# Re-pricing the planner of a four-layer graph kernel: copy times, transfer rate, a larger hold around LSTM steps, the last three batches closer together

## The chip, the cores and the metric

The kernel runs on one core of one Trainium2 chip. The metric is device time in microseconds from the first to the last instruction of one execution, as the median of repeated runs. A core has a tensor engine (PE; its weight loads are PEld in the profile), a vector engine (DVE), a scalar engine (ACT), a GpSimd engine (POOL) and a sync engine (SP), which here only issues transfers. Each engine works through its own list of instructions in order; semaphores order the engines among each other.

## The reference

There are 32 graphs (batches) of 512 nodes with 128 features each, and a symmetric 0/1 adjacency matrix per graph. Four layers follow each other, each reading `h = max(layernorm(x), 0)` and adding its result to `x`:

```
q, k, v = relu(h Wq + bq), relu(h Wk + bk), relu(h Wv + bv)
x = x + softmax_over_neighbours(q k^T) v                      # layer 0
dyn = conv1d(h[:, -128:]) + conv_b
A_norm = D^-1/2 (A + I) D^-1/2
x = x + sigmoid((A_norm h) lstm(dyn))                         # layer 1
for i in 0..3:                                                # layer 2
    src, dst = nodes ws + bs, nodes wd + bd
    nodes' = tanh([l2norm(A) src, nodes wn + bn, l2norm(A)^T dst] wu + bu)
    (layers 2 and 3 also read the earlier nodes)
x = x + nodes                                                 # end of layer 2
x = x + prelu(A (h W^T) + bias)                               # layer 3
```

The LSTM has 128 steps, each of which needs the state of the step before for all 32 graphs. It runs over the 128 features of the last 128 nodes, with 32 graphs side by side.

## The kernel before

`symmetric` does the work in three stages, each once per batch. `pass_1(b)` loads `x[b]` and the last 128 columns of the adjacency matrix, normalizes, transposes on PE (`ln_t`, L823), projects to k, q and v (L1098, L1114), writes k and h (`f_dkq`) and v (`f_dv`) to DRAM, computes attention for the last 128 nodes and the convolution that feeds the LSTM (L1166), whose result goes to `seq`. `lstm()` follows all 32 convolutions: per step three gates on PE (L1194, `f_z`), tanh on ACT (L1209), the cell update on DVE (L1216 to L1218), the fourth gate (`f_zo`), two more tanh on ACT and the new state on DVE (L1230), which the next step's gates read. `pass_2(b)` loads what pass 1 wrote and the other 384 columns, and computes attention for the other 384 nodes (L1248, L1257, L1266); it fills PE beside the LSTM. `rest(b)` does the remaining layers: it loads the whole adjacency matrix (`f_a`, 1 MB, two buffers), squares it to f32r with the degrees (L1318), aggregates (L1302), uses the LSTM's output (L1354, L1361), and then runs layer 2: four times a product (L1408, `f_py`), a split into two parts on ACT and DVE (L1284, L1285), an aggregation (L1302, `f_pa`), a multiply on DVE (L1415), a product (L1419) and tanh on ACT (L1423). Layer 3 is normalization, aggregation (`f_pg3` in the program), eviction (`f_gT`), a product (L1455), three elementwise instructions (L1458, L1459, L1461) and the store of `out` (L1463).

Layer 2 needs two transposes per batch: of its input (`f_xn_c` to `f_hT_c` or `f_T_c`) and of its output (`f_n4`). Batches in `MOVED` do them by transfer (`by_transfer`): a copy that takes each f32 apart into 16-bit halves (`f_hl`), a transposing transfer (L1059) and a copy that puts them together (`f_T`). The copies may run on ACT (L1053) or DVE (L1054). The other batches transpose on PE (L823) and evict.

The order of all this isn't written out. Each instruction, or short group of them, is given to `Plan` as an operation: the engines that it may run on with a price in microseconds each, a rank, what it reads and writes. `Plan.run` then lays the operations out one by one: on each engine it takes the operation that can start first, by rank among those that can start now; on operations with two engines it takes the one on which they end first. The prices thus set the order of every engine's list, and the choice between ACT and DVE. The times in the plan are used nowhere else: on the chip, each engine follows the list and waits for semaphores.

Three rules matter here:

- Ranks under 1000 are the LSTM's. When one is awaited on an engine (`expected`, `held`), a ready operation of another rank is passed over if it would end more than 0.1 us after the LSTM's operation could start.
- Operations of rank 30,000 and above (`rest`) get a due time: 12 per batch, minus what still lies behind the operation. The lower value goes first.
- A transfer occupies SP in the plan for `t_dma`, 0.1 us + its KB over a rate.

PSUM has 8 banks. A bank that takes a bias by a copy (`fill`) may need a marking matmul first (L910), depending on what the bank held. Sixteen warm-up matmuls of no use to the result (L898) stand at the start, and sixteen more after the last batch's transposes.

Of the kernel before, what the change touches and what calls it, by code (L numbers as in the profile page):

```python
# [520 lines left out]
class Plan:  # L521
# [67 lines left out]
    def run(self, tc, queues):  # L589
# [14 lines left out]
        for o in ops:  # L604
            if o.rank >= self.last:
                k, sub = divmod(o.rank - self.last, 10)
                o.rank = self.last + 12 * k + 200.0 - (min(behind[o], 60) if sub == 5 else behind[o] + (70 if sub == 2 else 0.0))
        free = {}
# [62 lines left out]
        while done < len(ops):  # L671
            best = None
            for e, cands in pools.items():
                first = None
                held = expected.get(e)
                for rank, no, o in cands:
                    r = room(o)
                    if r is None:
                        continue
                    if r:  # L680
                        r += self.HOP
                    s = max(free[e], o.ready[e], r)
                    if len(o.engines) > 1:
                        mine = s + o.engines[e][0]
                        if any(max(free[x], o.ready[x], r) + o.engines[x][0] < mine - 1e-9 for x in o.engines if x != e):
                            continue
                    if rank < self.URGENT:
                        held = s
                    elif held is not None and s < held < s + o.engines[e][0] - 0.1:
                        continue  # L690
                    if first is None or s < first[0] - 1e-9:
                        first = (s, o)
                        if s <= free[e] + 1e-9:
                            break
# [35 lines left out]
def symmetric(ctx, tc, x, adj, weights, cols, rows, lstm_b, prelu_a, out, fail):  # L730
# [20 lines left out]
    FOLDS = (4, 7, 10, 13)  # L751
    MOVED = range(3, B - 2)
    T_HALVES = 0.8
    TURN = 32
# [33 lines left out]
    def t_mm(n):  # L788
        return max(0.222, n * 0.001676)
# [12 lines left out]
    def t_dma(kb):  # L802
        return 0.1 + kb / 280.0

# [240 lines left out]
    def by_transfer(rank, src, c, tag, name):  # L1045
# [5 lines left out]

        def move(dst, src, r, w):
            return plan.op({"ACT": (T_HALVES, lambda: nc.scalar.copy(dst(), src())),  # L1053
                            "DVE": (1.05, lambda: nc.vector.tensor_copy(dst(), src()))}, rank, [r], [w])  # L1054

        apart = new("xn", (P, NT, 2, P), f"f_hl_{name}", U16)
        move(lambda: apart.t, lambda: halves(src()), c, apart)
        turned = new("gs", (P, 2 * NT, P), f"f_hT_{name}", U16)
        sent = plan.op({"SP": (1.3, lambda: nc.sync.dma_start_transpose(out=turned.t, in_=apart.t.rearrange("p t h n -> p (t h n)")))}, rank,  # L1059
                [apart], [turned], gap=3.0)  # L1060
        whole = new(tag, (P, N), f"f_T_{name}")
        move(lambda: halves(whole.t), lambda: turned.t.rearrange("p (t h) n -> p t h n", h=2), turned, whole)
        return whole, sent
# [110 lines left out]
    def lstm():  # L1174
# [23 lines left out]
        for t in range(T):  # L1198
# [7 lines left out]
            if t:  # L1206
                PE(R, 0.68, lambda z=z, k=k, t=t: states(z, k, (0, 1, 2), t), [], [z], after=last)
            th = new("th", (P, 4, B), f"f_th_{t}")
# [15 lines left out]
            if t:  # L1224
                PE(R, 0.23, lambda zo=zo, ko=ko, t=t: states(zo, ko, (3,), t), [], [zo], after=last)
            ACT(R, 0.13, lambda th=th, zo=zo, ko=ko: nc.scalar.activation(th.t[:, 3, :], zo.t[:, ko, 0, :], AF.Tanh), [zo],
# [80 lines left out]
    def rest(b, lw_after):  # L1307
# [79 lines left out]
        turned_d = new("dt", (P, TURN), f"f_dT_{b}")  # L1387
        DVE(R + 1, 0.18, lambda: nc.vector.transpose(turned_d.t, flat(dinv.t)), [dinv], [turned_d])
        ddi = plan.fixed(dram.tile([NT, P], FP, tag=f"i{b}", name=f"f_ddi_{b}"))
# [11 lines left out]
        for i, nch in enumerate(L2_CHUNKS):  # L1401
# [3 lines left out]
            def sent(py=py, i=i, nch=nch):  # L1405
                for j in range(NT):
                    for c, n in enumerate(CHUNKS[i]):
                        nc.tensor.matmul(py.t[:, j, :], nodes[n].t[:, bass.ts(j, P)], wf[:, W_F[i] + c, 0, :], start=False,  # L1408
                                         stop=(c == nch - 1), skip_group_check=True)
            PE(R, 4 * nch * t_mm(P), sent, [nodes[n] for n in CHUNKS[i]], [py])  # L1410
            parts = split(R, py, f"{b}_{i}")
# [182 lines left out]
```

## Time and profile before

| | |
|---|---|
| timed runs, median of 3 | 1375.77 us (1375.0 to 1376.33) |
| the profiled run | 1372.96 us, span of the profile 1371.2 us |
| TensorE clock granted, mean | 0.997 |
| PE in pass 1, first warm-up to the start of the last convolution's last matmul | 4.9 to 185.2 us |
| LSTM, first gates' tanh to last state | 187.8 to 497.0 us |
| last product of pass 2 on PE | 587.4 us |
| last matmul | 1361.3 us |
| end of the last vector instruction | 1363.7 us |

The page's first part gives each engine's busy time, its share of the span and its instructions. The windows view gives the same by stretches of time: start and end, length, busy time of PE, PEld, DVE, ACT and POOL with instructions, the granted clock, the DMA engines' share and GB/s. The ends of matmuls are modelled, so in some places the starts of neighbouring records tell more than durations. The waits view names who waited, on whose account, for how long in total, how often and for how long at most.

```
PE   8999999999999999999999999999999999999995
DVE  7888866666666678777777777677677677675753
ACT  5565644455444465666776777677677677675541
GB/s 246 244 262 245 261 266 262 262 163 183 164 147 153 166 156 165 157 155 106 144 132 131 142 128 131 154 123 127 150 139 120 148 133 130 147 131 78 66 35 27
```

These are rows of the page's second part: the span in 40 slices of 34 us, each digit the busy share in tenths.

### The profile page before, as it was taken

To read this page: it belongs to the slowest core of one execution; us is meant where nothing else is said; L and a number is where in the kernel's file an instruction comes from. 1 tells how busy PE (TensorE), PEld (TensorE's weight loads), DVE (VectorE), ACT (ScalarE), POOL (GpSimd) and SP (SyncE) were. 2 spreads that over 40 slices of the span, in tenths; PEclk is the share of its full clock that TensorE was granted. 3 is DMA by queue.
4 is the path that set the end of the run, shared out by engine and by line. 5 is a ranking of instruction groups with operands and counts; after the bars stand their busy time and mean duration, and the time that the engine had idled before them with its cause. 6 is when DMAs were issued, how large, how long until landed. Compare 5 with 4: busy or idle time off the path is not lost. (4 is left out here: it accounts for less than half of the span.)

```text
span 1371.2 us, 24258 instructions
## 1 busy us (share of the span) xinstructions
PE 1339.3 (98%) x8022; PEld 1079.1 (79%) x8024; DVE 976.3 (71%) x3259; ACT 824.8 (60%) x1958; POOL 370.5 (27%) x689
## 2 busy tenths in 40 slices
PE   8999999999999999999999999999999999999995
PEld 6888888888888877888778787787787787886873
DVE  7888866666666678777777777677677677675753
ACT  5565644455444465666776777677677677675541
POOL 4555411111010133333223233232232232231200
PEclk9999999999999999999999999999999999999998
DMA  7777888855545556764565565755765665753310
GB/s 246 244 262 245 261 266 262 262 163 183 164 147 153 166 156 165 157 155 106 144 132 131 142 128 131 154 123 127 150 139 120 148 133 130 147 131 78 66 35 27
DMA packets 284008, 215.22 MB, mean 157 GB/s; under 512 B 133464, under 2 KB 246368, under 8 KB 283872
## 3 DMA queue, kind: packets, MB, share of 16 engines
q1 hardware_dynamic: 266976, 196.79, 52.3%
q0 software_dynamic: 16896, 16.78, 7.8%
q8 instruction: 65, 1.06, 0.3%
q14 instruction: 71, 0.58, 0.1%
HBM read 125.84 MB, written 56.75 MB: 133 GB/s over the span
## 5 line engine op out<-in xcount | busy, mean ns | idle before, releaser
L1302 PE MATMUL f_pa<-f_ar,f_y 128*128 128x512 f32 x1024 | 284.3, 416 | 0.7 <-ACT f_y L1284 0.7
L1302 PEld LDWEIGHTS f_pa<-f_ar,f_y 128*128 128x128 f32 x1024 | 189.3, 189 | 60.5 <-issue 21.7
L1408 PE MATMUL f_py<-f_wf,f_n 128*128 128x128 f32 x1280 | 174.2, 276 | 0.8 <-ACT f_n L1423 0.8
L1408 PEld LDWEIGHTS f_py<-f_wf,f_n 128*128 128x128 f32 x1280 | 162.9, 192 | 13.9 <-issue 6.2
L1419 PE MATMUL f_pa<-f_n,f_wf 128*128 128x512 f32 x320 | 154.6, 598 | 2.1 <-DVE f_pa L1415 1.5
L1423 ACT ACTIVATE f_n<-f_pa,f_bcol 128x512 f32<-128x512 f32 x128 | 87.8, 686 | 81.5 <-PE f_pa L1419 81.3
L1376 POOL DMA_DIRECT2D f_das<-f_ar x32 | 30.8, 962 | 358.9 <-DVE f_ar L1345 358.1
L1285 DVE TENSOR_TENSOR f_y<-f_py,f_y 128x512 fp32r<-128x512 f32 x128 | 87.3, 683 | 36.5 <-ACT f_y L1284 36.0
L1194 PEld LDWEIGHTS f_z<-f_seq,f_w 128*128 128x128 f32 x762 | 95.7, 192 | 22.0 <-DVE f_seq L1230 20.7
L1415 DVE TENSOR_TENSOR f_pa<-f_pa,f_inv 128x512 f32<-128x512 f32 x128 | 87.5, 693 | 34.3 <-PE f_pa L1302 34.3
L1266 PEld LDWEIGHTS f_po<-f_v,f_e 128*128 128x128 f32 x768 | 99.7, 192 | 14.8 <-issue 0.5
L1266 PE MATMUL f_po<-f_v,f_e 128*128 128x129 f32 x768 | 107.9, 279 | 0.0
L1345 DVE TENSOR_TENSOR f_ar<-f_ar,f_ident 128x512 fp32r<-128x512 f32 x64 | 43.7, 683 | 88.5 <-PE f_pg L1302 78.8
L1194 PE MATMUL f_z<-f_seq,f_w 128*128 128x32 f32 x762 | 101.0, 270 | 2.2 <-DVE f_seq L1230 1.1
L1026 ACT ACTIVATE f_xn_c<-f_x,f_sh_c,f_rs_c 128x128 f32<-128x128 f32 x167 | 71.2, 486 | 50.0 <-DVE f_sh_c L1034 50.0
L1257 PE MATMUL f_s<-f_q,f_kq 128*128 128x384 f32 x256 | 99.7, 501 | 0.0
L1419 PEld LDWEIGHTS f_pa<-f_n,f_wf 128*128 128x128 f32 x320 | 55.8, 190 | 50.5 <-issue 37.0
L1284 ACT CAST f_y<-f_py 128x512 fp32r<-128x512 f32 x128 | 74.1, 579 | 29.7 <-PE f_py L1408 25.5
L1277 POOL COPY f_ln<-f_mv_r 128x3 f32<-128x3 f32 x32 | 10.5, 330 | 287.1 <-DVE f_mv_r L1008 287.1
L828 ACT ACTIVATE f_gT<-f_pg 128x512 f32<-128x512 f32 x60 | 36.0, 600 | 80.4 <-PE f_pg L1302 80.4
L1209 ACT ACTIVATE f_th<-f_z 128x96 f32<-128x96 f32 x128 | 32.0, 250 | 83.0 <-PE f_z L1194 80.8
L1318 ACT ACTIVATE f_ar<-f_a 128x512 fp32r<-128x512 f32 x128 | 79.5, 624 | 2.7 <-DMA f_a<-in_adj_dram 2.7
(205 smaller groups left out, 3024.7 us busy)
## 6 DMA issues: line engine op xcount, KB each, us to landing
f_a<-in_adj_dram SPq DMA_DIRECT2D x32, 1024.0 KB
f_a<-in_adj_dram SPq DMA_DIRECT2D x32, 768.0 KB
f_das<-f_ar POOLq DMA_DIRECT2D x32, 512.0 KB, 5.1
f_dkq<-f_kh SPq DMA_DIRECT2D x32, 448.0 KB
f_kq<-f_dkq SPq DMA_DIRECT2D x32, 448.0 KB
f_dv<-f_v SPq DMA_DIRECT2D x32, 258.0 KB
f_v<-f_dv SPq DMA_DIRECT2D x32, 258.0 KB
f_x<-in_x_dram SPq DMA_DIRECT2D x32, 256.0 KB
```

Of the source, the lines that this page charges most:

```text
L1026: nc.scalar.activation(xn.t[:, t, :], xc.t[:, t, :], AF.Relu, bias=shift(t), scale=rstd(t))
L1194: nc.tensor.matmul(z.t[:, k, i, :], w[:, W_HH + q, :], seq[:, t - 1, :], start=False, stop=True, skip_group_check=True)
L1257: PE(R, t_mm(NR), lambda s=s, j=j: nc.tensor.matmul(s.t, kq.t[:, bass.ts(j, P)], q.t, start=True, stop=True), [kq, q], [s])
L1266: PE(R, t_mm(P), lambda t=t, j=j: nc.tensor.matmul(po.t[:, t, :], es[j].t[:, bass.ts(t, P)], v.t[:, j, :], start=(j == 0), stop=(j == NT - ...
L1284: ACT(rank, t_act(N), lambda: nc.scalar.copy(parts.t[:, :, 0, :], src.t), [src], [(parts, 0)])
L1285: DVE(rank, t_dve(N), lambda: nc.vector.tensor_sub(parts.t[:, :, 1, :], src.t, f32(parts.t[:, :, 0, :])), [src, (parts, 0)], [(parts, 1)])
L1302: nc.tensor.matmul(pg.t, parts.t[:, j, k, :], ar.t[:, j, :], start=(k == 0 and j == 0), stop=(k == 1 and j == NT - 1))
L1318: ACT(R, 0.62, lambda t=t: nc.scalar.activation(ar.t[:, t, :], a.t[:, t, :], AF.Square, accum_out=deg.t[:, t : t + 1]), [a], [(ar, t), (de ...
L1408: nc.tensor.matmul(py.t[:, j, :], nodes[n].t[:, bass.ts(j, P)], wf[:, W_F[i] + c, 0, :], start=False, stop=(c == nch - 1), skip_group_chec ...
L1415: before = DVE(R, t_dve(N), lambda pa=pa: nc.vector.tensor_mul(pa.t, pa.t, inv_row.t), [inv_row], [pa])
L1419: nc.tensor.matmul(pa.t, wf[:, W_F[i] + c, 1, :], nodes[n].t, start=False, stop=(c == nch - 1), skip_group_check=True)
L1423: ACT(R, 0.57, lambda pa=pa, n=n, i=i: nc.scalar.activation(n.t, pa.t, AF.Tanh, bias=bcol[:, i : i + 1]), [pa], [n])
```

## The change

The computation stays as it is, but for one batch more that transposes by transfer. What changes is the planner's input and two of its rules:

- in `Plan.run`, the due times of the last three batches are drawn together: 3 apart instead of 12;
- a ready operation may end up to 0.2 us, instead of 0.1, after an LSTM operation could start;
- `MOVED` takes in batch 2;
- the transfer rate is 315 KB per us instead of 280;
- the copies of `by_transfer` have prices of their own: 0.94 (ACT) and 0.62 (DVE) for taking apart, 1.25 and 0.66 for putting together, instead of 0.8 and 1.05 for both;
- four prices are set a little lower: the LSTM's gates (0.68 to 0.65, 0.23 to 0.22), a small DVE transpose (0.18 to 0.14), and the product L1408 (by 0.01).

One line (`T_HALVES`) goes, so lines after it stand one higher: L1302 of before is L1301 of after.

```diff
-                o.rank = self.last + 12 * k + 200.0 - (min(behind[o], 60) if sub == 5 else behind[o] + (70 if sub == 2 else 0.0))
+                o.rank = self.last + 12 * k - 9 * max(0, k - 28) + 200.0 - (min(behind[o], 60) if sub == 5 else behind[o] + (70 if sub == 2 else 0.0))
...
-                    elif held is not None and s < held < s + o.engines[e][0] - 0.1:
+                    elif held is not None and s < held < s + o.engines[e][0] - 0.2:
...
-    MOVED = range(3, B - 2)
-    T_HALVES = 0.8
+    MOVED = range(2, B - 2)
...
-        return 0.1 + kb / 280.0
+        return 0.1 + kb / 315.0
...
-        def move(dst, src, r, w):
-            return plan.op({"ACT": (T_HALVES, lambda: nc.scalar.copy(dst(), src())),
-                            "DVE": (1.05, lambda: nc.vector.tensor_copy(dst(), src()))}, rank, [r], [w])
+        def move(t_act, t_dve, dst, src, r, w):
+            return plan.op({"ACT": (t_act, lambda: nc.scalar.copy(dst(), src())),
+                            "DVE": (t_dve, lambda: nc.vector.tensor_copy(dst(), src()))}, rank, [r], [w])
...
-        move(lambda: apart.t, lambda: halves(src()), c, apart)
+        move(0.94, 0.62, lambda: apart.t, lambda: halves(src()), c, apart)
...
-        move(lambda: halves(whole.t), lambda: turned.t.rearrange("p (t h) n -> p t h n", h=2), turned, whole)
+        move(1.25, 0.66, lambda: halves(whole.t), lambda: turned.t.rearrange("p (t h) n -> p t h n", h=2), turned, whole)
...
-                PE(R, 0.68, lambda z=z, k=k, t=t: states(z, k, (0, 1, 2), t), [], [z], after=last)
+                PE(R, 0.65, lambda z=z, k=k, t=t: states(z, k, (0, 1, 2), t), [], [z], after=last)
...
-                PE(R, 0.23, lambda zo=zo, ko=ko, t=t: states(zo, ko, (3,), t), [], [zo], after=last)
+                PE(R, 0.22, lambda zo=zo, ko=ko, t=t: states(zo, ko, (3,), t), [], [zo], after=last)
...
-        DVE(R + 1, 0.18, lambda: nc.vector.transpose(turned_d.t, flat(dinv.t)), [dinv], [turned_d])
+        DVE(R + 1, 0.14, lambda: nc.vector.transpose(turned_d.t, flat(dinv.t)), [dinv], [turned_d])
...
-            PE(R, 4 * nch * t_mm(P), sent, [nodes[n] for n in CHUNKS[i]], [py])
+            PE(R, 4 * nch * t_mm(P) - 0.01, sent, [nodes[n] for n in CHUNKS[i]], [py])
```

## The prediction

> **What bounds the kernel now.** I read the page's busy line first, then the windows view cut at the stages, then the tensor engine's waits, then the timeline inside each stage.
>
> ```profile
> PE 1339.3 (98%) x8022; PEld 1079.1 (79%) x8024; DVE 976.3 (71%) x3259; ACT 824.8 (60%) x1958; POOL 370.5 (27%) x689
> ...
> 0.00:187.00 187.00, 175.10 (x1275) 149.96 (x1276) 156.86 (x693) 106.40 (x205) 89.23 (x242) 1.00 0.77 251
> 187.00:497.00 310.00, 307.77 (x2153) 260.68 (x2152) 194.81 (x900) 148.07 (x536) 42.23 (x81) 1.00 0.61 188
> 497.00:560.00 63.00, 61.29 (x340) 47.27 (x339) 49.99 (x161) 38.20 (x92) 25.35 (x42) 1.00 0.68 172
> 560.00:1240.00 680.00, 680.00 (x3662) 534.57 (x3661) 503.43 (x1322) 474.45 (x1025) 198.25 (x301) 1.00 0.62 136
> 1240.00:1335.00 95.00, 94.04 (x502) 72.78 (x501) 56.74 (x148) 49.98 (x90) 12.92 (x20) 1.00 0.30 59
> 1335.00:1372.00 37.00, 21.08 (x103) 13.80 (x102) 14.42 (x39) 7.69 (x13) 2.53 (x4) 0.87 0.09 25
> ```
>
> TensorE (PE) is full from 560 to 1240 us, so only two things count: work taken from it, and time it loses elsewhere. Busy time hides small losses, so I took, for each kind of matmul record, the median distance from its start to the next start (0.112 us for a 128-column record, of which an f32 matmul has two; 0.43 for 512 columns f32, 0.232 for fp32r) and summed: 1318.6 us of work. The span is 1371.2, so 52.6 us are lost: 4.9 before the first matmul, 14.3 in the rest of pass 1 (to 187 us), 12.4 in the LSTM (187 to 497), 2.1 from there to 1240, 9.0 from 1240 to the last matmul, 9.9 after its start. The change can win only from these.
>
> ```profile
> PE f_pk L1098 <- ACT f_kh L828: 4.0, 7, 0.7
> ```
>
> In pass 1 the largest loss is this: transposes, their eviction, and the projection that reads it stand next to each other on PE. By start times it is 5.3 us.
>
> ```profile
> 343.19 0.76 PE L1194 MATMUL f_z<-f_seq,f_w 128*128 128x32 f32 x6
> ...
> 345.18 0.19 DVE L1230 SCALAR_TENSOR_TENSOR f_seq<-f_th,f_tcn 128x32 f32<-128x32 f32 x1
> ...
> 345.42 0.86 PE L1194 MATMUL f_z<-f_seq,f_w 128*128 128x32 f32 x6
> ```
>
> An LSTM step needs 2.23 us from its gates to the next step's. Where PE stands with less work than that between two steps, it waits for the rest.
>
> ```profile
> 1351.75 0.66 PE L823 MATMUL f_n4T<-f_ident,f_n 128*128 128x128 f32 x4 [0.78 <-ACT f_n L1423]
> ...
> 1357.58 2.11 PE L1302 MATMUL f_pg<-f_ar,f_xp_d 128*128 128x512 f32 x8 [1.71 <-ACT f_xp_d L1292]
> ...
> 1362.93 0.75 DVE L1461 SCALAR_TENSOR_TENSOR f_x<-f_neg,f_minus_alpha,f_x 128x512 f32<-128x512 f32 x1
> ```
>
> The last batch runs alone: 5.8 us from its transposes to its last aggregation, 6.1 more to the last vector instruction, 7.5 for the store to the end of the span.
>
> **What the Trainium skill says.** Perfetto Trace Analysis, Identifying the Most-Contended Engine: matmul occupancy is a poor measure of headroom, since pipelined matmuls overlap in the trace. This trace agrees: the page's mean for L1302 is 416 ns, its starts are 232 ns apart. TensorE: Matmul & The Clock Gate, Architectural detail: ScalarE and VectorE queues are strict FIFO. So a copy that waits for a transfer holds up what stands behind it; below. ScalarE: Activation LUTs, What ACT_TABLE_LOAD costs: an activation with immediates takes 186 ns + 0.833 ns per element, 1.04 us for 1024. The copy out of a normal layout agrees (1040 ns), the copy back doesn't (1332):
>
> ```profile
> L1053 ACT COPY f_hl_d<-f_n x26: 1040/1046/1046, 685.7 to 1307.6; 128x1024 uint16<-128x1024 uint16 x26
> L1053 ACT COPY f_T_d<-f_hT_d x5: 1332/1347/1358, 663.9 to 1311.8; 128x1024 uint16<-128x1024 uint16 x5
> L1054 DVE COPY f_T_d<-f_hT_d x22: 742/754/918, 691.8 to 1221.0; 128x1024 uint16<-128x1024 uint16 x22
> ...
>   DMA f_hT_d<-f_hl_d: 2.4, 4
>   DMA f_hT_c<-f_hl_c: 1.3, 3
> ```
>
> The last two lines are waits of DVE at these copies.
>
> **The change, part by part.** It edits a planner's prices, so what counts is the order that results. I set the instruction orders of the two programs side by side and weighed each matmul with the distances above.
>
> *Work on PE.* Batch 2 loses its 8 transposes (168 become 160): 8 x 0.109 = -0.9 us. Two marking matmuls of L910 come in (2 become 4), each with a weight load, at the warm spacing 0.215: +0.4. Sum -0.4. Batch 2's four added copies and two transfers lie beside a full PE.
>
> *Copies.* Of the 112 copies, 105 go to DVE and 7 to ACT (before: 47 and 61 of 108). With evictions and normalizations that swap engines too (DVE +19 ReLU and +21 plain evictions at 0.69, -27 normalizations at 0.34, -6 fills at 0.68) DVE gets 58 x 0.72 + 40 x 0.69 - 13 = +56 us, ACT about -60. DVE's share in the full stretch goes from 74% to about 80%. I price this at nothing, hidden by PE; bounds: 0 to +8 us (0.3 us for each of 28 moved batches), and no gain, since PE loses nothing there.
>
> *Transfer rate 315.* The loads of pass 2 for batches 0 and 1 now stand inside pass 1, so that bytes ahead of the load of x 31 rise from 37.6 to 40.0 MiB. PE uses them: 171.2 us of work stand ahead of the last convolution, instead of 166.0, the added 5.2 being pass-2 work. The places with under 0.9 us of other work between a batch's transposes and its projection fall from 9 (missing together 5.8 us, measured 5.3) to 4 (missing 2.7): -3.1 at best. Against it: at the 251 GB/s of this window 40.0 MiB pass by 167 us, and x 31 is used at 171 after some 4.5 us of statistics and normalization, so up to 3 us of waiting can come in at the end. I take -1.5; bounds -3.5 to +4. On SP, the new loads stand behind the writes of their sources and ahead of batch 13's writes.
>
> *Hold 0.2 and step prices.* More ready products go ahead of a step. PE work between consecutive steps rises from 2.33 us in the mean to 2.50. Summing what each of the 126 gaps lacks to 2.30 us gives 7.8 us before (start times show about 7.5 lost there) and 2.5 after; to 2.25, 5.7 and 1.5. So -4.2 to -5.3; I take -4.8. The LSTM gets longer: it starts with 5.9 us more PE work ahead of it and spans 21.6 us more, so it ends some 17 to 20 us later. Behind its end wait the transposes of its output (L1354) alone. The first stands at 493.7 us of PE work, after the last step at 491.7, and pass-2 products reach to 553: PE keeps other work. Bounds: -6 (all of it) to +1.
>
> *Last three close.* Layer 2 of batches 29, 30 and 31 starts at 1200, 1223 and 1245 us of PE work, instead of 1216, 1251 and 1275. The four layers of 31 now interleave with 30, 29 and 28. I checked every dependent pair of the last twelve batches on PE against its latency in the tail: 0.9 us from a product to the aggregation of its first part, 1.6 to the second, 0.8 from an aggregation to the product after its multiply and from there to the next layer. Before, five pairs of batch 31 lack 6.1 us together (start times show 6.2 lost there); after, one lacks 0.6. Behind the last transposes come 8.1 us of PE work, of which 2.9 are warm-ups, which leaves enough for the 5.8 us that the normalization needs; but DVE now has 2.9 us of other batches' work ahead of it, and the fill of batch 30's bank stands before it, so I add 0.6. Sum -5.0; bounds -7 to +1, the last if the loads of adjacency matrices, now closer together with two buffers, come late. The 13.6 us after the last aggregation starts stay.
>
> Sum: -0.4 + 0 - 1.5 - 4.8 - 5.0 = -11.7. Against the profile's own 1371.2 that is 1359.5; the median of the timed runs is 4.6 above that span (1375.77), and I take the difference over: **1364 us**.
>
> **Rivals.** *The transfers take the head's part* (17%): pass 1 already moves 251 GB/s, and later windows show no more than 267. For it: 6% more bytes in the same time. Against: DVE waited for x only 3.7 us in pass 1, and batch loads run ahead. With +4 instead of -1.5: 1369.5.
> *The LSTM's gain turns into other waits* (10%): a step held 0.2 us on PE, ACT and DVE in turn ends later, and batch 0 begins later. For it: 17 us of delay. Against: 60 us of pass-2 work remain. With 0 in place of -4.8: 1369.
> *Slower, by DVE's queue* (8%): each copy back waits at DVE for its transfer, and the multiply of L1415 behind it for as long; PE in its fixed order then stops. Place: the 28 moved batches, 600 to 1300 us. Before, 44 such copies on DVE cost it 3.7 us of waiting. The gains are gone at 11.7/28 = 0.42 us of PE time per batch; slower by more than 0.2% from 0.52. At 0.8 us, -11.7 + 22.4: 1386.
> *The change hardly does anything* (5%): the order differs, but PE's losses only move; 1374.
>
> **How the numbers follow.** 60% for the forecast, whose own spread is 1359 to 1369. With the two small rivals the range is 1357 to 1371; it leaves out the slower case and most of the last. A measurement of this kernel can tell about 0.2%, 2.75 us, from no change. Faster: 60 + 17 + 9 = 86%; same 6%; slower 8%.
>
> **What would show it.** PE at 40.0 of 40 between 560 and 1240 as before; the last LSTM step at about 512 to 517 instead of 497; PE's waits for the steps (L1194) down by 4 us or more; no idle over 1 us on PE between 1335 and the last transposes; these at about 1343. DVE copies at L1053 with over 10 us of waits for transfers, or PE idle in the full stretch, would make it wrong.

## The result, and the profile after

The changed kernel takes 1354.86 us in the median of four executions (1354.18 to 1355.54), the kernel before beside it 1376.05 (1375.0 to 1378.04). The ratio is 0.9844, 95% interval 0.9827 to 0.9861: 21.2 us less, where 11.7 were forecast. The direction was right; the size was short by nearly half, and 1354.86 lies below the range of 1357 to 1371. The two profiled executions are 1371.2 and 1352.8 us long, 18.4 us apart. The rest of the difference is in the choice of the profile before: its execution was one of the shorter ones (1372.96 us; medians of the same kernel in the experiments below are 1373.3 to 1375.1).

The page's busy line and the windows view of the changed kernel, with the columns of before:

```profile
PE 1329.0 (98%) x8016; PEld 1078.1 (80%) x8018; DVE 1004.6 (74%) x3315; ACT 782.5 (58%) x1905; POOL 374.2 (28%) x689
...
0.00:187.00 187.00, 179.49 (x1315) 154.39 (x1316) 155.90 (x703) 110.10 (x215) 91.57 (x245) 1.00 0.86 272
187.00:497.00 310.00, 309.61 (x2193) 265.59 (x2193) 202.20 (x917) 152.47 (x539) 47.70 (x93) 1.00 0.61 190
497.00:560.00 63.00, 60.72 (x341) 47.97 (x340) 49.73 (x153) 39.43 (x102) 20.78 (x30) 0.97 0.61 133
560.00:1240.00 680.00, 677.55 (x3630) 532.63 (x3629) 531.42 (x1375) 434.20 (x966) 200.07 (x301) 1.00 0.63 137
1240.00:1335.00 95.00, 94.75 (x508) 73.15 (x508) 58.80 (x159) 42.51 (x79) 13.81 (x21) 1.00 0.16 34
1335.00:1372.00 37.00, 6.83 (x38) 4.40 (x36) 6.57 (x12) 3.78 (x7) 0.32 (x1) 0.89 0.09 24
```

Read it against the windows of before row by row. Pass 1 holds 179.5 us of PE instead of 175.1 and moves 272 GB/s instead of 251. The LSTM's row gains 1.8 us of PE. Two rows get worse: 497 to 560, and 560 to 1240, where PE was full before. Work moves from ACT to DVE in that stretch, as forecast, but less of it: DVE has 28 us more (over the whole span too, by the busy line), against a forecast of 56, and ACT 40 less (42 over the span), against about 60.

Busy time hides small losses, so I made the same sum as in the prediction, from start to start. All times are what PE loses in us. The table also gives it for most of the experiments that follow, so that they can be read against it; the windows are cut at 187, 500, 600 and 1240 us (the last LSTM steps of some kernels, up to 509 us in the changed one, fall in the window from 500). A row is one execution.

```
                work    before first  to 187  187-500  500-600  600-1240  to last  after last  span
                on PE   matmul                                            matmul   matmul starts
before          1318.6  4.9           14.3    12.3      1.6       0.5      9.0      9.9        1371.2
after           1316.8  4.9            7.2     4.2      7.6       0.3      1.4     10.4        1352.8
after_again     1316.8  4.8            8.1     4.7      7.2      -0.1      1.5     10.1        1352.9
rate_alone      1316.5  4.9            9.7    13.7      5.4       0.1      7.1     10.2        1367.6
hold_alone      1317.2  5.0           15.2     8.1      8.2       1.6      7.1     10.1        1372.2
rank_alone      1318.7  4.9           15.6    12.2      5.3       1.0      1.8      9.9        1369.5
copy_alone      1319.1  5.1           17.2    12.5      1.6      -0.9      7.6      9.8        1371.9
rate_undone     1316.2  4.7           15.9     5.2     12.2       1.1      1.5     10.2        1367.1
hold_undone     1317.2  4.8            7.3    12.9      5.2       1.1      1.2     10.5        1360.2
steps_undone    1316.8  4.8            7.2     9.5      9.4      -0.1      1.4     10.2        1359.2
rate_350        1317.2  4.9           21.8     5.9     10.1      -0.4      1.4     10.1        1371.0
```

The first two rows tell where the 18.4 us are: 1.8 less work, 7.1 in pass 1, 8.1 in the LSTM, 7.6 at the end; and 6.0 given back between 500 and 600 us. What stands behind the last matmul's start is 0.5 longer. The next lines are those that answer to the prediction's.

PE's waits in pass 1, changed kernel (who waited, for whom: us, times, longest):

```profile
PE f_pk L1097 <- ACT f_kh L827: 1.7, 3, 0.7
```

Seven waits of 4.0 us have become three of 1.7. An LSTM step, from the timeline of the changed kernel (start, duration, engine, line):

```profile
346.18 0.85 PE L1193 MATMUL f_z<-f_seq,f_w 128*128 128x32 f32 x6
...
348.23 0.19 DVE L1229 SCALAR_TENSOR_TENSOR f_seq<-f_th,f_tcn 128x32 f32<-128x32 f32 x1 [0.35 <-ACT f_tcn L1228]
...
348.69 0.75 PE L1193 MATMUL f_z<-f_seq,f_w 128*128 128x32 f32 x6
```

The step itself is as fast as it was: 2.05 us from the gates' start to the new state, before 1.99 us between the answering starts (343.19 to 345.18). But PE comes back to it 0.46 us after the state began, later than before (0.24), because it had other work to finish. The last gates start at 508.0 us and the last state ends at 509.5 (before 495.7 and 497.2); the forecast had the last step at 512 to 517.

PE's waits between 497 and 602 us, where time is given back, first the kernel before, then the changed one:

```profile
PE f_py L1408 <- DVE f_py L918: 0.9, 1, 0.9
PE f_pa L1419 <- DVE f_sh_c L1034: 0.6, 1, 0.6
PE f_xt_c L823 <- ACT f_n L1423: 0.2, 1, 0.2
```
```profile
PE f_po L1265 <- DMA f_v<-f_dv: 1.5, 1, 1.5
PE f_py L1407 <- ACT f_py L913: 1.3, 1, 1.3
PE f_xt_c L822 <- ACT f_xn_c L1025: 0.8, 1, 0.8
PE f_pa L1418 <- DVE f_pa L1414: 0.2, 1, 0.2
```

The end, from the timeline of the changed kernel:

```profile
1329.70 0.60 PE L822 MATMUL f_n4T<-f_ident,f_n 128*128 128x128 f32 x4
1330.06 1.17 PE L1301 MATMUL f_pg<-f_ar,f_xp_d 128*128 128x512 f32 x4
...
1338.36 2.10 PE L1301 MATMUL f_pg<-f_ar,f_xp_d 128*128 128x512 f32 x8
...
1344.03 0.75 DVE L1460 SCALAR_TENSOR_TENSOR f_x<-f_neg,f_minus_alpha,f_x 128x512 f32<-128x512 f32 x1
```

Before, the last transposes waited 0.78 us and stood 5.8 us ahead of the last aggregation. Now they wait for nothing, another batch's aggregation starts 0.36 us behind them, and the last aggregation comes 8.7 us later, after work that stood in front of the transposes before. From the start of that aggregation to the end of the span it is 14.4 us, where the prediction let 13.6 stay.

The copies (line, engine, us in total and mean ns; idle time before them) and DVE's wait for the transfer, changed kernel:

```profile
L1053 DVE COPY f_T_c<-f_hT_c 128x1024 uint16<-128x1024 uint16 x27 | 20.3, 751 | 0.2 <-DMA f_hT_c<-f_hl_c 0.2
L1053 DVE COPY f_T_d<-f_hT_d 128x1024 uint16<-128x1024 uint16 x27 | 20.2, 748 | 1.8 <-DMA f_hT_d<-f_hl_d 1.8
```

With 54 instead of 44 copies back in its queue DVE waits 2.0 us for transfers in all, less than before (3.7). The slower rival, which needed more than 0.5 us of PE time for each batch, is out.

### The profile page after: what moved, and what is told of

Read it like the earlier page. It is cut to its first block, busy times and chain, and to the rows that moved or that the text cites. A ratio compares the mean times of both kernels' runs of the same rounds, so it can differ in the third digit from the quotient of the medians.

```text
span 1352.8 us, 24316 instructions
## 1 busy us (share of the span) xinstructions
PE 1329.0 (98%) x8016; PEld 1078.1 (80%) x8018; DVE 1004.6 (74%) x3315; ACT 782.5 (58%) x1905; POOL 374.2 (28%) x689
## 5 line engine op out<-in xcount | busy, mean ns | idle before, releaser
L1301 PE MATMUL f_pa<-f_ar,f_y 128*128 128x512 f32 x1024 | 304.5, 431 | 0.0
L1301 PEld LDWEIGHTS f_pa<-f_ar,f_y 128*128 128x128 f32 x1024 | 190.2, 189 | 73.6 <-issue 40.1
L1407 PE MATMUL f_py<-f_wf,f_n 128*128 128x128 f32 x1280 | 174.1, 275 | 0.0
L1407 PEld LDWEIGHTS f_py<-f_wf,f_n 128*128 128x128 f32 x1280 | 164.8, 192 | 8.7 <-ACT f_n L1422 1.0
L1375 POOL DMA_DIRECT2D f_das<-f_ar x32 | 36.0, 1126 | 367.6 <-DVE f_ar L1344 348.6
L1193 PEld LDWEIGHTS f_z<-f_seq,f_w 128*128 128x128 f32 x762 | 96.7, 191 | 15.6 <-DVE f_seq L1229 12.7
L1414 DVE TENSOR_TENSOR f_pa<-f_pa,f_inv 128x512 f32<-128x512 f32 x128 | 88.3, 692 | 17.4 <-PE f_pa L1301 17.2
L1025 ACT ACTIVATE f_xn_c<-f_x,f_sh_c,f_rs_c 128x128 f32<-128x128 f32 x199 | 86.1, 495 | 11.9 <-DVE f_sh_c L1033 11.9
L1380 DVE SCALAR_TENSOR_TENSOR f_junk<-f_a,f_aT 128x1024 bf16<-128x1024 f32 x64 | 78.3, 1223 | 9.7 <-DMA f_aT<-f_das 8.1
L1260 DVE TENSOR_TENSOR f_e<-f_e,f_a 128x384 f32<-128x384 f32 x128 | 68.5, 551 | 14.4 <-ACT f_e L1259 13.4
```

Source lines behind the costliest of these rows:

```text
L1025: nc.scalar.activation(xn.t[:, t, :], xc.t[:, t, :], AF.Relu, bias=shift(t), scale=rstd(t))
L1193: nc.tensor.matmul(z.t[:, k, i, :], w[:, W_HH + q, :], seq[:, t - 1, :], start=False, stop=True, skip_group_check=True)
L1301: nc.tensor.matmul(pg.t, parts.t[:, j, k, :], ar.t[:, j, :], start=(k == 0 and j == 0), stop=(k == 1 and j == NT - 1))
L1380: nc.vector.scalar_tensor_tensor(junk, flat(a.t[:, 2 * k : 2 * k + 2, :]), 1.0, flat(aT.t[:, 2 * k : 2 * k + 2, :]), OP.mult, OP.not_equal ...
L1414: before = DVE(R, t_dve(N), lambda pa=pa: nc.vector.tensor_mul(pa.t, pa.t, inv_row.t), [inv_row], [pa])
```

## The experiments

Each kernel was timed beside the kernel before; ratios are to that, with 95% intervals, and a gain in us behind a ratio is the ratio times the median of before. "Alone" is one part of the change put into the kernel before, "undone" is one part taken back in the changed kernel. "Slower than the changed kernel" sets a median against 1354.26, the median of the changed kernel timed again below on another chip; by the ratios to the kernel before, the three differences of 11.8, 8.1 and 13.0 us would be 13.2, 9.8 and 13.7. PE's order in pass 1 depends on the rate only, and its order at the very end (from 1307 us on in the changed kernel) on the due times only, so there the traces can be read by window; between 187 and 600 us the parts mix.

**The transfer rate alone.** `kb / 280.0` becomes `kb / 315.0`.

> The kernel before with the transfer rate 315 instead of 280 and nothing else. The matmul order of pass 1 is then that of the changed kernel: 5.2 us more other work ahead of the last convolution, 12.5 instead of 14.5 MiB of transfers ahead of the load of x 12, 40.0 instead of 37.6 MiB ahead of x 31. Theory 1 (the prediction): only the places where transposes and their projection are neighbours count, less a little waiting for transfers: -1.5 us, at most -3.5. Theory 2 (the earlier x loads also end waits in the middle of pass 1, and the transfers go faster when they are asked for earlier): the whole loss of pass 1 falls from 14 to about 7 us, -7 us; the later LSTM, 6 us, gives back at most 1. Rival (pass 1 isn't affected by the rate, the gain there comes from another part): 0.

Measured: 1369.96 us against 1375.08, ratio 0.9965 (0.9949 to 0.9981), -4.8 us. The loss in pass 1 is 9.7 us in its trace. The four traces above that have the pass-1 order of before lose 14.3, 15.2, 15.6 and 17.2 there. It is the rate, and it brings much more than -1.5. The total is short of theory 2's -7; the trace loses 1.4 us more in the LSTM and 3.8 more between 500 and 600 us than that of before, though there other traces with the list of before lose up to 5.4.

**The hold alone.**

```diff
-                    elif held is not None and s < held < s + o.engines[e][0] - 0.1:
+                    elif held is not None and s < held < s + o.engines[e][0] - 0.2:
```

> The kernel before with the hold 0.2 instead of 0.1 and nothing else; the gates keep their prices of 0.68 and 0.23. Work between steps rises from 2.33 to 2.43 us in the mean (2.50 in the changed kernel), what the gaps lack to 2.30 us falls from 7.8 to 4.8 us. Theory 1 (the steps' gain follows what the gaps lack, and work behind the LSTM hides its delay): waits of the gates -3 us, total -3. Theory 2 (the delay of the LSTM by 13 us is partly paid between 497 and 600 us): gates -3, loss between 500 and 600 us +2 to +3, total 0. Rival (the loss between 500 and 600 us of the changed kernel belongs to the copies or to the rate): gates -3, nothing there, total -3.

Measured: 1372.99, ratio 0.9983 (0.9975 to 0.9991), -2.3 us. The LSTM loses 8.1 instead of 12.3 us, 4.2 less, more than the 3 expected; between 500 and 600 us the trace loses 8.2. Theory 2 has the right terms, both larger than it said; its total of 0 is outside the interval (-1.2 to -3.4 us), in which theory 1's -3 lies. The last gates of this kernel stand at 505.5 us, 9.8 later than before.

**The due times alone.**

```diff
-                o.rank = self.last + 12 * k + 200.0 - (min(behind[o], 60) if sub == 5 else behind[o] + (70 if sub == 2 else 0.0))
+                o.rank = self.last + 12 * k - 9 * max(0, k - 28) + 200.0 - (min(behind[o], 60) if sub == 5 else behind[o] + (70 if sub == 2 else 0.0))
```

> The kernel before with the last three batches due 3 apart instead of 12 and nothing else. Dependent pairs of batch 31 lack 0.6 instead of 6.1 us. Theory 1 (the prediction): 9.0 us of loss between 1240 us and the last matmul become about 4, -5.0 us. Theory 2 (as the changed kernel's trace reads): the loss there falls to about 1.5, -7 us. Rival (the gain at the end needs the copies on DVE as well): under -3.

Measured: 1369.81, ratio 0.9954 (0.9940 to 0.9967), -6.3 us. The loss after 1240 us falls to 1.8: theory 2, and the copies on DVE aren't needed for it. The trace shows another thing too. Its list on PE is that of before up to 1172 us of work, and still it loses 5.3 us between 500 and 600 us instead of 1.6. PE's and ACT's waits between 497 and 602 us in this kernel:

```profile
PE f_xt_c L823 <- ACT f_n L1423: 2.7, 1, 2.7
...
ACT f_ar L1318 <- DMA f_a<-in_adj_dram: 3.3, 1, 3.3
```

ACT stands at a squaring whose matrix hasn't landed, for 3.3 us; what is behind it on ACT waits, and PE with it. In the profile of before that squaring waits 0.9 us, and the same place of PE (537.9 us) loses 0.4. So about 2.4 us of the distance between the profiled execution of before and its median can be a load that comes in time in one execution and not in another.

**The prices of the copies alone.**

```diff
-        move(lambda: apart.t, lambda: halves(src()), c, apart)
+        move(0.94, 0.62, lambda: apart.t, lambda: halves(src()), c, apart)
...
-        move(lambda: halves(whole.t), lambda: turned.t.rearrange("p (t h) n -> p t h n", h=2), turned, whole)
+        move(1.25, 0.66, lambda: halves(whole.t), lambda: turned.t.rearrange("p (t h) n -> p t h n", h=2), turned, whole)
```

> The kernel before with the new prices of the copies and nothing else (3 to 29 as before in the set of moved batches). 76 copies on DVE instead of 47. Theory 1 (the prediction): PE hides them, 0 (-1 to +1). Theory 2 (the loss between 500 and 600 us of the changed kernel comes from the copies in DVE's queue): +4 to +6, all of it in that window. Rival (copies waiting in DVE's queue stop PE in the full stretch): +5 and more between 600 and 1300 us.

Measured: 1373.32, ratio 0.9987 (0.9980 to 0.9995), -1.8 us: within 0.2%, so hardly to be told from nothing, and if anything a gain. No window of the full stretch loses anything. Theory 1.

**The prices of the gates undone.** In the changed kernel 0.65 and 0.22 go back to 0.68 and 0.23.

> The changed kernel with the two prices of the gates back at 0.68 and 0.23. Work between steps falls from 2.50 to 2.43 us in the mean, what the gaps lack to 2.30 us rises from 2.5 to 5.3 us, the last step stands 9.2 us earlier. Theory 1 (the two prices are a part of the hold: what the gaps lack decides): waits of the gates +2.8 us, total +2.8 less up to 1 in the window after the LSTM: 1357. Theory 2 (the earlier end of the LSTM saves between 500 and 600 us what the gaps lose): 1355. Rival (the last 5 us, which the four parts done alone don't explain, come from other edits): under +1.

Measured: 1366.09 (1361.02 to 1369.84), ratio 0.9944 (0.9928 to 0.9960). That is 11.8 us slower than the changed kernel (1354.26 in its repeated timing, below): a good deal more than any theory said. The trace is of its fastest execution, 1361.02 us. It shows 5.3 us more in the LSTM (9.5 instead of 4.2, expected 2.8) and 1.8 more between 500 and 600 us. What the slower executions add isn't in a trace. These two edits of 0.03 and 0.01 us, of which I had made nothing but a part of the hold, are worth at least as much as the hold's own edit by the medians; by the traces they are about equal, 6.4 and 7.4 us of span. They can account for the four parts done alone adding up to only -15.2 us, but the gates' prices were not run alone, nor were batch 2 in `MOVED` and the two other small prices.

**The hold undone.** In the changed kernel 0.2 goes back to 0.1.

> The changed kernel with the hold 0.1, prices of the gates as changed. Work between steps 2.335 us in the mean, lack 8.0 us instead of 2.5, the last step 21 us earlier. Theory 1 (what the gaps lack decides, the delay of the LSTM costs nothing): +5.5, 1360. Theory 2 (the delay costs part of it between 500 and 600 us): gates +5.5, 500 to 600 us -3 to -6, total 0 to +2.5: 1356. Alone on the kernel before, the hold (without the prices) brought 2.3 us of 3.0.

Measured: 1362.32, ratio 0.9919 (0.9905 to 0.9933), 8.1 us slower than the changed kernel. The LSTM loses 8.7 us more, 500 to 600 us 2.4 less. Both theories have a half: the gates count for more than 5.5, and the earlier end goes with a smaller loss behind it.

**The rate undone.** In the changed kernel 315 goes back to 280.

> The changed kernel with the rate 280 again. Pass 1 has the matmul order and the order of transfers of the kernel before. Theory 1 (the rate does the gain of pass 1, done alone 4.8 us): loss to 187 us 14 to 17 us instead of 7, gates lack 3.6 instead of 2.5 us: +7 to +9, 1362 to 1364. Rival (the gain of pass 1 needs the other edits too, since the rate alone brought less than 7): +4 to +5, 1359.

Measured: 1367.3, ratio 0.9948 (0.9933 to 0.9963), 13.0 us slower than the changed kernel, more than theory 1. Pass 1 loses 15.9 us, as it said; the LSTM 1.0 more than with 315. Another 4.6 us are lost between 500 and 600 us, which no theory had.

**The rate at 350.** In the changed kernel `kb / 315.0` becomes `kb / 350.0`.

> The changed kernel with the rate 350 instead of 315. Transposes and their projection are neighbours in 3 places instead of 5 (lack 2.2 instead of 2.6 us), 8.4 us more other work stand ahead of the last convolution than before, instead of 5.2; ahead of the load of x 12 stand 14.0 MiB, as many as before the change nearly (12.5 in the changed kernel, 14.5 before), ahead of x 16 20.5 instead of 17.0, ahead of x 31 42.4 instead of 40.0. Theory 1 (the gain in pass 1 is the distance of the pairs): loss to 187 us 7 or a little less, 1354. Theory 2 (about half of it is that the loads of x 12 and its neighbours come in time): the waits between 55 and 90 us come back, +3 to +4, 1358. Theory 3 (the transfers reach their ceiling): loss at the end of pass 1, from 140 to 187 us, +2 or more, with x late.

Measured: 1373.44, ratio 0.9996 (0.9986 to 1.0005): the whole gain is gone, though the pairs of theory 1 are as far apart as ever. Pass 1 loses 21.8 us. Windows of pass 1 from 40 to 60 us (DMA share and GB/s last), first the kernel before, then the changed one, then this one:

```profile
40.00:60.00 20.00, 19.88 (x153) 17.65 (x152) 17.05 (x66) 11.05 (x22) 8.65 (x27) 1.00 0.71 244
```
```profile
40.00:60.00 20.00, 19.85 (x149) 17.13 (x148) 18.49 (x91) 13.13 (x26) 15.61 (x38) 1.00 0.82 251
```
```profile
40.00:60.00 20.00, 18.12 (x133) 15.38 (x133) 15.96 (x72) 12.42 (x24) 8.17 (x24) 1.00 0.95 288
```

The engines of the transfers are at 0.95 of their time here. DVE's waits in pass 1 of this kernel name what is late:

```profile
DVE f_st_a L1005 <- DMA f_x<-in_x_dram: 9.1, 8, 2.3
...
DVE f_kh L831 <- DMA f_dkq<-f_kh: 5.2, 2, 3.5
```

The loads of x (3.7 us of waiting before, 5.2 after) and the buffers of k, which come free only when the write to DRAM has gone. The loss is spread over all of pass 1, with 2.5 us at 178: what theories 2 and 3 name, but 14.6 us more than in the changed kernel, where the two together foresaw 5 to 6. Over the 187 us the transfers move 270 GB/s, no more than the 272 of the changed kernel, with the same share of 0.86. That fits a ceiling near which the changed kernel already works. It isn't shown: with 350 more bytes also stand ahead of a load of x in SP's list (14.0 instead of 12.5 MiB at x 12), which makes it late without any ceiling, and I ran no kernel with fewer bytes at this rate.

**Less of POOL's work in pass 1.** In the kernel before, the halving of the LSTM's weights touches one column.

```diff
-        nc.gpsimd.tensor_scalar_mul(w[:, W_HH + q, :], w[:, W_HH + q, :], 0.5 * half)
+        nc.gpsimd.tensor_scalar_mul(w[:, W_HH + q, 0:1], w[:, W_HH + q, 0:1], 0.5 * half)
...
-            nc.gpsimd.tensor_scalar_mul(w[:, W_IH + q, :], w[:, W_IH + q, :], half)
+            nc.gpsimd.tensor_scalar_mul(w[:, W_IH + q, 0:1], w[:, W_IH + q, 0:1], half)
```

> The kernel before, with every list of instructions in the same order, but the seven instructions of POOL that halve the LSTM's weights (L928, L930; 128x128, 0.55 us each, 61.5 to 69 us) touch one column only: 3.5 us less of POOL's work in the middle of pass 1. The weights are then not halved, so the LSTM computes something else. In the changed kernel these instructions stand at 48.8 to 56.7 us. Theory 1 (a good part of the gain of pass 1 that the distance of the pairs doesn't explain, 4 us between 40 and 80 us, is this work in POOL's queue ahead of the normalizations): loss from 40 to 80 us 5.2 to 5.6 becomes 2 to 3, total -2.5 to -3.5. Theory 2 (only the distances of the pairs and the transfers count): 0, loss from 40 to 80 us above 4.5.

Measured: 1373.49, ratio 0.9996 (0.9985 to 1.0006). The loss between 40 and 80 us is 4.5 us, instead of 5.0 to 5.6 in the five traces with the same order in pass 1. POOL's work explains about 1 us at most; theory 1 falls.

**The check of symmetry made lighter.** Between 500 and 600 us I suspected the check that runs beside layer 2: POOL writes the matrix to DRAM, SP transposes it by transfer, DVE compares. For batches 0 to 5 it covers 128 of 512 rows and columns here (write, transfer and compares alike), so this kernel leaves out the rest of the check for them:

```diff
-        POOL(R + 2, 1.4, lambda: nc.gpsimd.dma_start(das.t.rearrange("(t p) j -> p t j", p=P), f32(ar.t)), [ar], [das], gap=6.0)
+        POOL(R + 2, 1.4, lambda: nc.gpsimd.dma_start(das.t[:P, :P], f32(ar.t[:, 0, :P])) if b < 6 else nc.gpsimd.dma_start(das.t.rearrange("(t p) j -> p t j", p=P), f32(ar.t)), [ar], [das], gap=6.0)
...
-        plan.op({"SP": (3.0, lambda: nc.sync.dma_start_transpose(out=aT.t, in_=das.t))}, R + 2, [das], [aT], gap=4.0)
+        plan.op({"SP": (3.0, lambda: nc.sync.dma_start_transpose(out=aT.t[:, 0, :P], in_=das.t[:P, :P]) if b < 6 else nc.sync.dma_start_transpose(out=aT.t, in_=das.t))}, R + 2, [das], [aT], gap=4.0)
...
+                if b < 6:
+                    nc.vector.scalar_tensor_tensor(junk[:, :P], a.t[:, 0, :P], 1.0, aT.t[:, 0, :P],
+                                                   OP.mult, OP.not_equal, accum_out=viol[:, b, k : k + 1])
+                    return
```

> The changed kernel, with every list in the same order, but the check that the adjacency matrix is symmetric (a copy to DRAM by POOL, the transposing transfer that holds SP for 2 to 4 us, two compares of 1.2 us on DVE, L1380) covers only 128 of 512 columns and rows for batches 0 to 5. Theory 1 (what is lost between 500 and 600 us, 7.6 us, comes from this work in the queues of SP, DVE and POOL, and from the buffers of the adjacency matrix that it holds): 3 us or less, total -4 to -5. Theory 2 (it comes from the latency of the first batches' chains when the LSTM's end comes late and little other work is left): 6 us or more, total 0 to -1.

Measured: 1351.73 us; the changed kernel on the same chip 1354.26. The loss between 500 and 600 us is 3.5 instead of 7.2 us, and the median is 2.5 us lower: theory 1 for one half of the loss. That is one trace against two of the changed kernel (7.6 and 7.2), and the ranges of the timed runs overlap, so it points to the check more than it proves it. One of the places, in SP's list and on PE, first the changed kernel, then this one:

```profile
566.08 0.39 SPq L1312 DMA_DIRECT2D f_a<-in_adj_dram  x1
566.52 0.49 SPq L1244 DMA_DIRECT2D f_v<-f_dv  x1
...
574.04 2.92 PE L1265 MATMUL f_po<-f_v,f_e 128*128 128x129 f32 x24 [1.55 <-DMA f_v<-f_dv]
```
```profile
563.84 0.39 SPq L1312 DMA_DIRECT2D f_a<-in_adj_dram  x1
564.27 0.49 SPq L1244 DMA_DIRECT2D f_v<-f_dv  x1
...
571.75 2.84 PE L1265 MATMUL f_po<-f_v,f_e 128*128 128x129 f32 x24
```

A load of v stands in SP's list behind a load of an adjacency matrix. In the changed kernel v lands 7.5 us after its issue (566.52 to 574.04), and PE had been there 1.55 us earlier. With the lighter check the load is issued earlier against PE's work: PE comes 7.5 us after it (564.27 to 571.75), 1.5 us later than it did in the changed kernel, and doesn't wait.

**The changed kernel again**, on the chip of the last two:

> The changed kernel itself, once more on the chip of the other two. All theories: 1354 to 1356, losses by window as in its first trace within 1 us, unless the loss between 500 and 600 us differs from run to run as in the kernel before (1.6 in its trace, 5.3 in the kernel with the rank alone, which has the same order there); then up to 1358.

Measured: 1354.26 (1351.82 to 1355.78), ratio 0.9848 (0.9830 to 0.9866), -20.9 us. Losses by window within 1 us of the first trace. The 7.2 us between 500 and 600 us are there again, though not all at the same places.

**The check later.** The due time of the check in the changed kernel: `70 if sub == 2` becomes `40 if sub == 2`.

> The changed kernel with the compares of the adjacency check due 30 us later (70 becomes 40 in the due time), so that they stand less often ahead of the first batches' own steps; all work is done. Pass 1 and the LSTM keep their order. Theory 1 (of the 3.7 us that the lighter check saved between 500 and 600 us, the place in the queues is what counts): loss there 7.4 becomes 4 to 6, total -1.5 to -3: 1352. Theory 2 (the check also holds the two buffers of the adjacency matrix, and a later compare delays the next load): the loss stays or grows by up to 4, and PE loses in the full stretch too: 1354 to 1360.

Measured: 1355.16, ratio 0.9857 (0.9837 to 0.9877); loss between 500 and 600 us 8.2. Nothing is gained: it fits theory 2 in its mild form, and 8.2 isn't far from the 7.2 and 7.6 of the changed kernel.

**One half of the check at a time.** Two more kernels split the lighter check: in the first only DVE's compares are cut to 128 rows and columns, in the second only the write and the transfer (the compares keep their length).

> The changed kernel, every list in the same order, but DVE's two compares of the adjacency check (1.2 us each) cover 128 of 512 columns and rows for batches 0 to 5; the copy to DRAM and the transposing transfer stay whole. The lighter check as a whole brought the loss between 500 and 600 us from 7.4 to 3.5 us. Theory 1 (the compares in DVE's queue ahead of the first batches' steps): 3.5 to 4.5 us, total -2.5. Theory 2 (the transposing transfers in SP's queue and the buffers): 7 us, total 0.

> The changed kernel, every list in the same order, but the copy of the adjacency matrix to DRAM and its transposing transfer cover 128 of 512 columns and rows for batches 0 to 5; DVE's compares keep their 1024 elements per partition each, reading the same 128 columns again and again. Theory 1 (the compares in DVE's queue): loss between 500 and 600 us 7 us, total 0. Theory 2 (the transposing transfers, 2 to 4 us in SP's queue ahead of the loads of v and of the adjacency matrix): 3.5 to 4.5 us, total -2.5.

Measured: 1353.22 and 1353.9 us, ratios 0.9850 (0.9832 to 0.9868) and 0.9854 (0.9837 to 0.9870); losses between 500 and 600 us 6.8 and 6.9. Neither half brings what both bring, in one trace each. In both traces PE still waits for v (1.37 and 0.87 us). That fits a chain in which the matrix's buffer comes free only after the transfer and the compares, but it's read from the order of the lists, not tested further.

## Why the prediction was right or wrong

The sum was -11.7; the traces say -18.4. Of the 6.7 us between them the transfer rate makes 5.6, the last batches 2.1 and the work on PE 1.4; the hold and the delay behind it, 3.3 too small and 6.0 too favourable, make up for 2.7 (0.3 stands elsewhere or is rounding). That these two partly cancel is luck. The predicted time, 1364 us, misses by 2.5 us more for another reason: the prediction carried over the 4.6 us by which the median of before stood above its profile's span, and for the changed kernel that is 2.1.

*Work on PE: -0.4, measured -1.8.* The medians of the spacings differ by 0.7 us between traces with the same list (1316.8 to 1317.5 for kernels with the changed list), so about half of this is within that error and I don't read more into it.

*Copies: 0, held.* The prices alone cost nothing between 600 and 1240 us, and the changed kernel loses 0.3 us there with 105 of 112 copies on DVE. The reason given holds: PE hides them. The +56 us for DVE was too much, though. The copies came as counted; but of the evictions charged at 0.69 us most of those beyond the 21 plain ones are of 128x128 elements (L833, 24 more than before) and take 0.29.

*Transfer rate: -1.5, measured about -7.* This term failed most, in two steps. The first: I counted one kind of neighbours only, transposes and their projection. That part was right (-3.1 at best; measured by start times 5.25 to 2.52, -2.7). But the order at 315 also empties other kinds: a score product followed by a convolution (1.0 us to 0), transposes followed by a product with v (1.0 to 0), a product for v followed by the next transposes (0.7 to 0.1), and smaller ones; together 4.4 us. They were in the profile of before, as waits of under 1 us each. DVE's waits for x did not shrink (3.7 to 5.2 us), so it isn't earlier loads of x that brought the gain. The second: I took 251 GB/s as what the transfers can do and charged 1.6 us for it. The charge came to nothing: pass 1 now moves 272, so 251 was no limit. At 350 loads do come late and +14.6 us are lost, whether from a ceiling or from the order of SP's list. POOL's halvings, which stood in the way too, were worth about 1 us at most.

*Hold and step prices: -4.8, measured -8.1 in the LSTM.* The mechanism was right; the step that failed is the size of the loss that it can take away. I had summed what each gap lacks to 2.30 us, and let what that sum doesn't explain stand. A sum to 2.40, chosen after the traces, stands beside it; against the LSTM's measured loss:

```
                lack to 2.30   lack to 2.40   measured loss 187-500
before           7.8            12.5           12.3
rate_alone       8.2            13.5           13.7
hold_undone      8.0            13.1           12.9
steps_undone     5.3             9.3            9.5
hold_alone       4.8             8.3            8.1
rate_undone      3.6             6.2            5.2
rate_350         3.0             5.4            5.9
after            2.5             4.5            4.2
```

The sum to 2.40 us meets the total of eight kernels within 1 us, but not the places. In the trace of before the 49 gaps that hold less than 2.4 us of work lose 8.2 us, close to the 7.8 of the sum to 2.30; the rest is lost in gaps that hold more, 4.2 us in the 72 with 2.4 to 2.5. In the changed kernel the two parts are 2.0 and 2.4 us. So the short gaps gave 6.2 us (the sum said 5.3, and I took 4.8), and the gaps with work enough, whose loss I had assumed to stay, gave 1.7 more. Why those lose anything is open: in all 72 the other work stands behind the fourth gate, and the loss arises behind it too. The sign that I had named, PE's waits for the steps down by 4 us or more, can't be read from the waits view, which shows only 1.1 us of them before and 0.2 after; by start times the LSTM loses 8.1 us less.

*The delay: 0, measured +6.0 against the profile of before.* "PE keeps other work" failed, and the rival of gains that turn into other waits was right about the mechanism and wrong in size. By PE's work ahead of the last step, the kernels at 464 us lose 1.6, 1.6, 5.3 and 5.4 us between 500 and 600 us (the last is the kernel with less of POOL's work); those at 470, 5.2 and 5.4; those at 477 and later that do the whole check, 7.2 to 12.2, though not in the order of the delay. The other work is there; as I read the lists, the loads of the first batches of layer 2, their check and the last products of pass 2 now meet in the same 100 us, in lists that are strictly in order. Since kernels with the list of before vary from 1.6 to 5.4 there, about 2 to 6 us are given back. Half of the changed kernel's loss goes away with the lighter check, in one trace. Another 1.5 us are there in every trace of the changed list: the product L1407 directly behind the transposes (L822) that it needs, where ACT first evicts the transposes and then fills the product's bank (L913), which ends the wait. The rest stays open.

*Last three close: -5.0, measured -7.1* (-7.6 before the last matmul, +0.5 after it). The five pairs of batch 31 were right: by start times they lose 6.2 us before and 1.0 after, the latter at the product behind the last aggregation. The other losses after 1240 us, 2.8 us outside these pairs, fell to 0.4; I had left them standing, and that is the step that failed here.

Of the signs to look for: PE is at 677.55 of 680 us between 560 and 1240, not quite full, by one wait of 1.5 us for v and one of 0.9 for ACT (`f_xp_c`); no idle time over 1 us stands between 1240 and the last transposes. These come at 1329.7 instead of 1343. Half of that distance is the larger gain; most of the rest is a slip of mine, since 8.1 us of work behind the transposes and 13.6 us from the last aggregation on, counted back from the span of 1359.5, give 1338. Faster, at 86%, came true. The range didn't hold it: the rate and the last batches came out beyond the favourable ends of their bounds (-3.5 and -7), the LSTM without its delay too (-6), and I had let the bad ends weigh as much as the good ones.

## What to carry to other kernels

Where a list is laid out by a planner, account for every loss of the stretch that a change reorders, and not only for those with a name: an order with more distance between dependent instructions removes the nameless ones too. What the transfers moved in one order need not be what they can do: 251 GB/s looked like a limit here and 272 were possible; but a plan that assumed still more (350) lost more than the step from 280 to 315 had won. And a delay is free only if all lists have room where it ends, not just the engine that sets the time.

## What the runs showed of the hardware that I had not expected

- The core's transfers, reading and writing mixed, went at 272 GB/s over 187 us, and at 294 and 296 GB/s in windows of 20 us of the changed kernel (80 to 100 and 120 to 140 us), with the DMA engines at 0.86 to 0.91. Before, 251 had looked like a limit.
- Two executions with the same PE list up to 1172 us of work can differ by 3.7 us in one 100 us stretch, 2.4 of it at a place where ACT stands for a 1 MB load (the kernel before and the one with the due times alone).
- The granted clock fell shortly after PE had stood for two short waits (1.5 and 0.9 us): 0.89 between 520 and 525 us and 0.77 between 525 and 530 in the changed kernel. Six aggregation records in there start 0.43 us apart instead of 0.23, so the clock was at about half; what is missing from 1.00 in the two windows then makes some 3.4 us at half speed (an estimate from these figures). In the trace of the due times alone, around a wait of 2.7 us, 0.69 and 0.97 in two such windows (540 to 550 us) give 3.4 us as well. In the second trace of the changed kernel the same two waits leave the clock at 1.00, and the span is the same to 0.1 us.
